# Second attention of a two-layer transformer kernel: moving the expert pieces behind the score rounds and spacing the two router calls

## The chip, the core and the metric

The kernel runs on one core of a Trainium2 chip. The core has a matrix engine (PE, with its weight loads shown apart as PEld), a vector engine (DVE), an activation engine (ACT), a general engine (POOL) and a queue engine that issues most transfers (SP). Each works through its own list of instructions in order, and waits on semaphores for the others. The metric is the device time of one execution in microseconds, the median of several runs; lower is better.

## The reference, cut to what matters

Two layers, each an attention with 16 heads of width 8 and then a mixture of 8 experts, of which each token takes 2. There are 64 batches of 128 tokens of width 128, all in float32. The change is in the second layer:

```python
x = x + _L0_xattn_ref(_layernorm(x), fside_BxSxS_0, ctx_1024, ctx_1024, ...)
x = x + _L0_ffn_ref(_layernorm(x), ...)
x = x + _L1_xattn_ref(_layernorm(x), ctx_1024, ctx_1024, ...)
x = x + _L1_ffn_ref(_layernorm(x), ...)
...
# _L1_xattn_ref, 120 keys a batch
scores = jnp.einsum('bhqd,bhkd->bhqk', Q, K) / jnp.sqrt(jnp.asarray(d, Q.dtype))
attn = jax.nn.softmax(scores, axis=-1)
out = jnp.einsum('bhqk,bhkd->bhqd', attn, V)
...
# _L1_ffn_ref
logits = xf @ Wg.T + bg
top_gates, top_idx = jax.lax.top_k(logits, K)
top_gates = jax.nn.softmax(top_gates, axis=-1)
h = jax.nn.gelu(jnp.einsum('nd,erd->enr', xf, W1), approximate=False)
eout = SCALING * jnp.einsum('enr,edr->ned', h, W2)
sel = jnp.take_along_axis(eout, top_idx[:, :, None], axis=1)
out = jnp.sum(top_gates[:, :, None] * sel, axis=1)
```

## The kernel before, in words

All 64 batches stay in on-chip memory as 16 groups of 4 (`xg`, `GB = 4`, `NG = 16`). The kernel runs through three stages: the first attention with the first router beside it, the first layer's experts as a stage of sorted tiles (`tile_stage`, L934), and the second attention (`attention(1, ...)`, called at L1278), beside which the second layer's router and experts run. The order of instructions on PE, DVE, ACT and POOL is the order in which the Python code writes them (`manual_schedule`).

**One iteration of the second attention** (the loop at L484; 69 iterations for 64 batches, since the stages of a batch are spread over iterations) does, for different batches at once:

- `values` and `out1` (L408, L424): softmax weights times values for batch `it-3`, 16 matmuls in L417; ACT copies the result (`ov`, L426).
- `rounds(0, 1)` (L384): for batch `it` the score matmuls whose row maxima are wanted (L344, 16 of them, banks that DVE reduces in L356), woven with those of batch `it-2` in transposed form (L372, 8 of them, banks that ACT turns into exponentials in L380). Four banks go to DVE and four to ACT.
- `prep` (L303): in turn over four iterations, keys (L188), values and the turned input (L199, L165), queries (L269) of the next group.
- `out3`, `out2`, `out4` (L446, L433, L453): transposes and the output projection; between them DVE computes `rs` and `o` (L437, L439).
- `shift` (L397): two transposes of the maxima (L401), which DVE adds into the queries (L404), so that the next iteration's L372 and L380 work on shifted scores.
- `out5`, `ahead`, `norm_of`, `fetch_for`: residual adds and statistics on DVE (L458, L116, L117), and on POOL the normalization of coming groups (L144 to L156) and the gathers of the first layer's expert results (`yb`, L1157, two indirect transfers an iteration), which are added to `x` (L1169).
- Then `aside.call` twice in a row (L545, L546).

**PSUM** is one pool of 8 banks (L225). A matmul that opens a bank waits until the bank's last reader is done; which bank it gets follows from the order in which the code takes and gives them up.

**The router** (`Router`, L559) is three generators that are driven by `call`; a counter `t` goes up by one at each call, and each generator says at which `t` it is due again. `front` (L596) runs per group: at `2 * (4 g + made_at)` statistics and normalization on POOL, at `2 * (4 g + at)` four transposes on PE and one ACT copy (`turned`, L162), and one call later the four logit matmuls (L615) that read that copy, with a DVE copy of the logits (L619). With `when = (8, 9)` (L1147) the turn and the logits stand back to back at the end of iteration `4 g + 9`. `back` (L625) then takes top-2 and gates in small DVE steps, one step a call (L712, L652 to L684, L1203 and L1204).

**The experts** (`experts`, L1209) are a generator with four pieces a group. A: the gates transposed (L1218), copied by ACT, and four matmuls of 512 columns (L1225), whose banks ACT passes through Gelu (L1228; ACT then has to load another table, and the exponentials' table again before the next L380). B: 16 small matmuls that spread the gates over four banks (L1235), by which DVE multiplies `h` (L1240, four times 512 columns). C twice: 8 matmuls back to width 128 (L1246) and a DVE add (L1251), the second time with the transfer out. `Aside1.call` (L1258) steps the router and, at every second call, the experts: one piece an iteration, as the last thing in it. What is left after the loop is done in `rest` (L1265).

Of the kernel before, what the change touches and what calls it, by code (L numbers as in the profile page):

```python
# [28 lines left out]
E = 8  # L29
# [15 lines left out]
def transformer_kernel(ctx, tc, a, out):  # L45
# [24 lines left out]
    def load_const(name, shape, src):  # L70
        t = const.tile(shape, F32, name=f"c_{name}", tag=f"c_{name}")
        nc.sync.dma_start(t, src)
        return t
# [94 lines left out]
    norms = [Norm(n) for n in range(4)]  # L168
# [48 lines left out]
    def attention(layer, w, norm, first, aside):  # L217
# [5 lines left out]
        with ExitStack() as es:  # L223
# [34 lines left out]
            def prep_x(g):  # L258
                xnT = work.tile([D, GB * S], F32, name="xnT", tag="xnT", bufs=1)
                norm.turned(normed.pop(g), mtile(), xnT)  # L260
                xnTs[g] = xnT
                q4s[g] = work.tile([128, GB, NS, S], F32, name="q4", tag="q4", bufs=3)
# [3 lines left out]
            def prep_q(g, v):  # L266
                if v == 0:
                    pqs[g] = mtile()
                    nc.tensor.matmul(pqs[g], lhsT=w["wq"], rhs=xnTs[g], start=True, stop=True)  # L269
                pq = pqs[g]  # L270
                for i in range(2):
                    s = 2 * v + i
                    nc.scalar.activation(  # L273
                        q4s[g][:, :, s, :], pq.rearrange("p (b q) -> p b q", b=GB),
                        AF.Identity, bias=w["bq"][:, s : s + 1], scale=hmask[:, s : s + 1],
                    )

            def prep_k(g):
                keys_of(w, src[g], g, n0, mtile())

            def prep_v(g):
                values_of(w, src[g], g, n0, mtile())
# [20 lines left out]
            def prep(it, half):  # L303

                g, j = it // GB + 1, it % GB
                if not first:
                    if g == 1:
                        if (j, half) == (2, 1):
                            prep_v(1)
                        elif (j, half) == (1, 0):  # L310
                            prep_k(1)
                    elif g < NG:
                        pieces = (
                            (), (lambda: prep_k(g),),
                            (lambda: prep_v(g), lambda: prep_x(g)),
                            (lambda: prep_q(g, 0), lambda: prep_q(g, 1)),
                        )[j]
                        if half < len(pieces):
                            pieces[half]()
                    return  # L320
                if (it, half) == (0, 1):
                    norm_of(1)
                    prep_x(1)
                if (j, half) == (3, 1):
                    if g + 1 < NG:
                        prep_x(g + 1)
                elif g >= NG:
                    return
                elif j == 0 and it or it == 1:
                    prep_q(g, half)  # L330
                elif (j, half) == (2, 0):
                    prep_k(g)
                elif (j, half) == (2, 1):
                    prep_v(g)
# [49 lines left out]
            def round_(ba, bc, rnd):  # L384


                one, two = ((0, 2), (1, 3)) if rnd % 2 == 0 else ((1, 3), (0, 2))
                left = [max_bank(ba, ra, rnd // 2) for ra in one] if ba is not None else []
                right = [score_bank(bc, ra, rnd // 2) for ra in two] if bc is not None else []
                banks = [x for pair in zip(left, right) for x in pair] if left and right else left + right  # L390
                for u in range(2):
                    for parts, _ in banks:
                        parts[u]()
                for _, after_ in banks:
                    after_()
# [65 lines left out]
            def norm_of(g):  # L461
                if g < NG:
                    normed[g] = norm.normed(g)

                    nc.gpsimd.tensor_tensor(
                        xg[g], xg[g], w["bo"].unsqueeze(1).to_broadcast([S, GB, D]), ALU.add
                    )
# [16 lines left out]
            for it in range(B + (4 if first else 5)):  # L484
                def on(back, *steps):
                    b = it - back
                    if 0 <= b < B:
                        for f in steps:
                            f(b)

                def rounds(*which):
                    ba = it if it < B else None
                    bc = it - 2 if 0 <= it - 2 < B else None
                    for r in which:
                        if ba is not None or bc is not None:
                            round_(ba, bc, r)

                if first and it % GB == 2:
                    norm_of(it // GB + 2)
                if 2 <= it <= B + 1:  # L500
                    ps_[it - 2] = work.tile([128, nc_, 4, 512], F32, name="p", tag="p")
                on(3, lambda b: values(b, 0), lambda b: values(b, 1), out1)
                if it % GB == 0 and 0 < it // GB + 1 < NG:
                    if it:
                        loads(it // GB + 1)
                if it % GB == 2 and it // GB + 1 < NG:
                    context(it // GB + 1)
                rounds(0, 1)
                if first:

                    on(3, out2)
                    prep(it, 0)
                    rounds(2, 3)
                    on(1, shift)
                    on(3, out3)
                    aside.call(it, mtile)
                    on(4, out4, out5)
                    aside.ahead(it)
                    prep(it, 1)
                    aside.call(it, mtile)  # L520
                    aside.end(it, work, mtile)
                else:
                    if it < GB - 1:
                        prep_batch(it + 1)
                    prep(it, 0)
                    on(4, out3)
                    on(3, out2)
                    on(5, out4)
                    prep(it, 1)
                    on(1, shift)  # L530
                    on(5, out5)
                    aside.ahead(it)
                    if it == GB - 1 or it > GB and it % GB == 1:
                        norm_of(it // GB + 1)
                    if it == 1:

                        nc.gpsimd.tensor_tensor(
                            xg[0], xg[0], w["bo"].unsqueeze(1).to_broadcast([S, GB, D]), ALU.add
                        )
                    if it == GB - 1:  # L540
                        prep_x(1)
                        prep_q(1, 0)
                        prep_q(1, 1)
                    aside.fetch_for(it)
                    aside.call(it, mtile)  # L545
                    aside.call(it, mtile)  # L546
                ps_.pop(it - 3, None)
                yield
# [10 lines left out]
    class Router:  # L559
# [15 lines left out]
        def call(self, probe, mtile):  # L575
            self.mtile, self.probe = mtile, probe
            self.t += 1
            for k, gen in enumerate(self.gens):
                if self.due[k] <= self.t:
                    self.due[k] = next(gen, 1 << 30)  # L580
# [529 lines left out]
    rp = ctx.enter_context(tc.tile_pool(name="route", bufs=1))  # L1110
# [9 lines left out]
    wr1 = load_const("wgT", [D, E], a["wgT"])  # L1120
# [14 lines left out]
    class Aside1:  # L1135


        def __init__(self, pool):
            self.pool, self.got, self.b, self.xn = pool, {}, 0, None
            self.xnTs, self.gates, self.ready = {}, [], []  # L1140
            for k in range(2):
                t = pool.tile([S, QM, 32], F32, name=f"gates_{k}", tag=f"gates_{k}")
                nc.gpsimd.memset(t, 0.0)  # L1143
                self.gates.append(t)
            parts = [(2 * k, 2 * k + 1) for k in range(GA // 2)] + [(g,) for g in range(GA, NG)]
            self.router = Router(
                rp, 1, norms[3], E, wr1, logits1, self.weigh, self.xnT_of, parts, (8, 9)  # L1147
            )
            self.work = self.experts()

# [105 lines left out]
                    yield  # L1256

        def call(self, it, mtile):  # L1258
            self.mtile = mtile
            self.router.call(None, mtile)  # L1260
            self.half = not getattr(self, "half", True)
            if self.half:
                next(self.work, None)

        def rest(self, mtile):  # L1265
            self.mtile = mtile
# [101 lines left out]
```

## Time and profile before

| what | value |
|---|---|
| median of 5 runs (lowest, highest) | 1624.65 us (1619.04, 1628.79) |
| profiled execution, its own time | 1631.8 us |
| its span, first to last instruction | 1630.0 us |
| mean granted clock of the matrix engine | 0.954 |
| second attention with its tail, about | from 1000 us to the end |
| stretch 1140 to 1580 us: PE, DVE, ACT, POOL busy | 406.20, 295.99, 250.89, 192.34 us |
| the same stretch: granted clock | 0.94 |

The profile is of one execution. Its views name an instruction by engine, line and operation, with its tiles written as "out <- in" and its shapes as partitions by elements. A list of waits puts idle time of an engine down to what ended it. A timeline gives start, length and, in brackets, the idle time ahead of an instruction and what released it. A table of windows gives the busy time of each engine in a stretch, then the clock that was granted to the matrix engine (PEclk, 1.00 is full speed). Matrix instructions are pipelined, and their ends are modelled.

### The profile page before, as it was taken

How to read it: one execution, taken by the hardware profiler on the slowest of the kernel's cores; microseconds unless marked ns; L12 is line 12 of the kernel's file. 1: busy time of each engine (PE TensorE's matmuls, PEld its weight loads, DVE VectorE, ACT ScalarE, POOL GpSimd, SP SyncE). 2: the span in 40 equal slices, each digit the busy share in tenths (PEclk: the TensorE clock that was granted, in tenths of full speed). 3: DMA queues.
4: the chain of work that ended last, by engine and by line, in shares of the span. 5: the costliest groups of instructions: out<-in, count | busy, mean ns of one | idle time of the engine just before them, and what ended most of it. 6: DMA issues, size and time to landing. Idle time of an engine off the chain costs nothing.

```text
span 1630.0 us, 44916 instructions
## 1 busy us (share of the span) xinstructions
PE 1474.4 (90%) x18156; PEld 1176.0 (72%) x18156; DVE 1059.9 (65%) x2923; ACT 838.7 (51%) x1722; POOL 641.5 (39%) x1211
## 2 busy tenths in 40 slices
PE   5999999999999998879999994788989899899997
PEld 3777777777776776868888883567767676677765
DVE  4778887878788875545544442467665666667854
ACT  3666665656565655423333332445555565556652
POOL 5124265555555545640000005575454555543200
PEclk9999999999999999999999995798998898999998
DMA  7411122222222221667766751110001111110000
GB/s 190 104 45 45 45 62 57 60 58 59 59 76 56 76 51 58 181 173 211 198 193 190 193 169 43 28 36 24 27 28 27 28 35 26 35 30 15 15 8 27
DMA packets 124130, 123.91 MB, mean 76 GB/s; under 512 B 47122, under 2 KB 106514, under 8 KB 122002
## 3 DMA queue, kind: packets, MB, share of 16 engines
q1 hardware_dynamic: 115730, 103.71, 23.8%
q0 software_dynamic: 8192, 17.32, 3.5%
q8 instruction: 144, 2.36, 0.6%
q14 instruction: 64, 0.52, 0.1%
HBM read 97.31 MB, written 23.67 MB: 74 GB/s over the span
## 4 chain that ended last, share of the span: by engine, by line
PE 76%; DVE 7%; ACT 5%; DMA 4%; issue 3%; POOL 2%; SPq 1%; another core or an unknown queue 1%; ACTq 0%; POOLq 0%; DVEq 0%
PE bank L372 15%; PE bank L417 12%; PE bank L344 12%; PE bank L997 9%; PE bank L1225 4%; PE bank L1246 4%; PE bank L1010 3%; DVE nm L356 3%; PE bank L401 2%; DMA q<-xs 2%; PE bank L433 2%; PE bank L269 2%; PE bank L615 2%; ACT p L380 2%; DMA vc<-xs 2%
## 5 line engine op out<-in xcount | busy, mean ns | idle before, releaser
L356 DVE TENSOR_REDUCE nm<-bank 128x2 f32<-128x496 f32 (+1 forms) x768 | 464.6, 663 | 244.4 <-PE bank L372 133.0
L372 PE MATMUL bank<-q,k 32*120 32x256 f32 (+1 forms) x3072 | 479.7, 417 | 13.0 <-ACT ov L426 4.8
L344 PE MATMUL bank<-k,q 32*128 32x248 f32 (+1 forms) x4096 | 463.6, 351 | 2.8 <-ACT q L298 1.1
L380 ACT ACTIVATE p<-bank 120x512 f32<-120x512 f32 (+1 forms) x768 | 402.9, 602 | 121.3 <-PE bank L372 78.0
L344 PEld LDWEIGHTS bank<-k,q 32*128 32x128 f32 x4096 | 361.9, 198 | 65.5 <-issue 28.2
L372 PEld LDWEIGHTS bank<-q,k 32*120 32x120 f32 (+1 forms) x3072 | 305.9, 186 | 41.5 <-DVE nm L356 15.4
L417 PE MATMUL bank<-p,v 128*32 128x128 f32 (+1 forms) x4096 | 199.5, 283 | 16.2 <-issue 13.1
L1002 DVE TENSOR_TENSOR p<-p,bank 128x256 f32<-128x256 f32 x213 | 88.1, 420 | 139.0 <-ACT p L1001 121.8
L426 ACT COPY ov<-bank 128x256 f32<-128x256 f32 x128 | 47.4, 371 | 236.9 <-PE bank L417 191.4
L417 PEld LDWEIGHTS bank<-p,v 128*32 128x32 f32 (+1 forms) x4096 | 122.8, 112 | 54.3 <-issue 33.8
L751 POOL DMA_INDIRECT xs<-xn,at x128 | 128.9, 1007 | 54.5 <-issue 30.6
L1157 POOL DMA_INDIRECT yb<-ys,back x128 | 123.7, 966 | 32.2 <-issue 28.0
L1001 ACT ACTIVATE p<-bank 128x256 f32<-128x256 f32 x213 | 80.7, 384 | 105.8 <-PE bank L997 103.0
L997 PE MATMUL bank<-q 128*128 128x256 f32 x516 | 120.8, 384 | 2.9 <-ACT e L675 1.8
L404 DVE SCALAR_TENSOR_TENSOR q<-bank,c_smask,q 128x256 f32<-128x256 f32 x256 | 111.1, 475 | 10.3 <-remote 4.2
L417 PE MATMUL bank<-p,vc 120*32 120x128 f32 x2048 | 114.3, 273 | 2.3 <-issue 2.1
L156 POOL TENSOR_SCALAR xn<-x,mv,rstd 128x128 f32<-128x128 f32 x256 | 111.2, 447 | 11.1 <-PE bank L165 5.2
L144 POOL TENSOR_SCALAR rstd<-mv 128x4 f32<-128x4 f32 (+1 forms) x33 | 6.5, 198 | 273.6 <-DVE mv L117 187.6
L997 PEld LDWEIGHTS bank<-q 128*128 128x128 f32 x516 | 95.8, 192 | 14.8 <-ACT e L675 2.1
L1143 POOL MEMSET gates<- 128x256 f32 x2 | 0.6, 311 | 250.2 <-DMA ys<-q 250.2
L273 ACT ACTIVATE q<-bank,c_a_bq,c_hmask 128x512 f32<-128x512 f32 x124 | 89.7, 781 | 13.3 <-PE bank L269 13.3
L997 PE MATMUL bank<-vc 128*128 128x256 f32 x336 | 78.8, 385 | 0.0
(201 smaller groups left out, 2284.9 us busy)
## 6 DMA issues: line engine op xcount, KB each, us to landing
q<-in_w SPq DMA_DIRECT2D x43, 576.0 KB
vc<-in_w SPq DMA_DIRECT2D x28, 576.0 KB
vc<-in_ctx_v SPq DMA_DIRECT2D x16, 960.0 KB
k<-in_ctx_k SPq DMA_DIRECT2D x32, 240.0 KB
q<-xs SPq DMA_DIRECT2D x43, 128.0 KB
ys<-q SPq DMA_DIRECT2D x43, 128.0 KB
x<-in_x SPq DMA_DIRECT2D x16, 256.0 KB
kvT<-in_fsideT SPq DMA_DIRECT2D x16, 256.0 KB
```

The source lines that it names most:

```text
L156: nc.gpsimd.tensor_scalar(xn[:, j, :D], xg[g][:, j, :], self.mv[:, b, 0:1], self.rstd[:, b : b + 1], ALU.add, ALU.mult,)
L273: nc.scalar.activation(q4s[g][:, :, s, :], pq.rearrange("p (b q) -> p b q", b=GB), AF.Identity, bias=w["bq"][:, s : s + 1], scale=hmask[:, ...
L344: nc.tensor.matmul(pa[:, u, :], lhsT=q4s[g][r, j, s, :], rhs=k2[g % 2][r, s // 2, j, :], start=True, stop=True,)
L356: nc.vector.tensor_reduce(nm[b % 2].rearrange("q i (a s) -> q a i s", s=16)[:, 2 * ra + v : 2 * ra + v + len(slots) // 2, :, 0], pa.rearra ...
L372: nc.tensor.matmul(pb[:n, v * 256 : (v + 1) * 256], lhsT=k2[g % 2][r, v, j, k0 : k0 + n], rhs=q4s[g][r, j, 2 * v : 2 * v + 2, :].rearrange ...
L380: nc.scalar.activation(ps_[b][:n, c, ra, :], pb[:n], AF.Exp, scale=SCALE)
L404: nc.vector.scalar_tensor_tensor(q, pm, smask[:, v : v + 1], q, ALU.mult, ALU.add)
L417: nc.tensor.matmul(pav[32 * ra : 32 * ra + 32, v * S : (v + 1) * S], lhsT=vs[g % 2][c][:, j, 4 * v + ra, i, :], rhs=p[:n, c, ra, (2 * v + ...
L751: s = nc.gpsimd.indirect_dma_start(xs, bass.IndirectOffsetOnAxis(at[:, j, k : k + 1], 0), xn, None)
L997: nc.tensor.matmul(ph[:, u, :], lhsT=w[:, c, u * 128 : (u + 1) * 128], rhs=xT, start=True, stop=True)
L1002: nc.vector.tensor_tensor(hT[:, c, :], sa, ph[:, 1, :], ALU.mult)
L1157: nc.gpsimd.indirect_dma_start(y[:, k, b % 2, :], None, ys, bass.IndirectOffsetOnAxis(back[:, b, k : k + 1], 0),)
```

## The change

The expert piece is taken out of `Aside1.call` into a method of its own, `piece`, which is called once an iteration directly after the rounds, before `prep`. One of the two router calls moves to the middle of the iteration, between `out4` and the second half of `prep`; the other stays at the end. The router's two due times move by half an iteration, `(8, 9)` to `(8.5, 9.5)`: the normalization and the turn stay at the end of iterations `4 g + 8` and `4 g + 9`, and the logits come in the middle of iteration `4 g + 10`. All else is as it was.

```diff
                 else:
+                    aside.piece(mtile)
                     if it < GB - 1:
                         prep_batch(it + 1)
                     prep(it, 0)
                     on(4, out3)
                     on(3, out2)
                     on(5, out4)
+                    aside.call(it, mtile)
                     prep(it, 1)
                     on(1, shift)
                     on(5, out5)
...
                     aside.fetch_for(it)
-                    aside.call(it, mtile)
                     aside.call(it, mtile)
...
             self.router = Router(
-                rp, 1, norms[3], E, wr1, logits1, self.weigh, self.xnT_of, parts, (8, 9)
+                rp, 1, norms[3], E, wr1, logits1, self.weigh, self.xnT_of, parts, (8.5, 9.5)
             )
...
         def call(self, it, mtile):
+            self.router.call(None, mtile)
+
+        def piece(self, mtile):
             self.mtile = mtile
-            self.router.call(None, mtile)
-            self.half = not getattr(self, "half", True)
-            if self.half:
-                next(self.work, None)
+            next(self.work, None)
```

In the built order of PE's instructions, an iteration that ended "... out4, shift, turn, logits, piece A" becomes "values, rounds, piece A, prep, out3, out2, out4, logits, turn, shift", one iteration later; B, C and C follow in the three iterations after it, each directly behind the rounds. The number of instructions of each engine is the same, POOL's order is the same, and SP's is too. On DVE the multiplications of B and the adds of C now stand between the four reductions (L356) and `rs`, `o` and the shift (L437, L439, L404); before, they stood at the iteration's end. On ACT the Gelu of A stands directly behind the four exponentials instead of at the iteration's end.

## The prediction

> **What bounds the kernel now.** I read the page first, then tables of windows cut at the iterations of the second attention, then timelines and waits of single engines there.
>
> ```profile
> PE 1474.4 (90%) x18156; PEld 1176.0 (72%) x18156; DVE 1059.9 (65%) x2923; ACT 838.7 (51%) x1722; POOL 641.5 (39%) x1211
> ...
> PEclk9999999999999999999999995798998898999998
> ...
> PE 76%; DVE 7%; ACT 5%; DMA 4%; issue 3%; POOL 2%; SPq 1%; another core or an unknown queue 1%; ACTq 0%; POOLq 0%; DVEq 0%
> ```
>
> PE is busy for 90% and carries 76% of the chain that ended last, so what the change is worth is read from PE: its idle time, and stretches at a lower clock. The clock row is full until slice 24 and dips in the last 16 of 40, nearly all of them the second attention, which is changed. I cut that part at the first L417 of each iteration. A group takes four iterations, those of pieces A, B, C, C. An undisturbed group late in the stage:
>
> ```profile
> 1510.80:1521.90 11.10, 10.18 (x111) 6.83 (x110) 7.54 (x30) 7.71 (x15) 6.56 (x15) 1.00 0.08 26
> 1521.90:1529.00 7.10, 7.07 (x136) 6.11 (x135) 4.58 (x12) 4.96 (x9) 1.11 (x1) 1.00 0.00 0
> 1529.00:1536.90 7.90, 7.90 (x109) 6.56 (x109) 7.39 (x20) 5.01 (x10) 0.00 (x0) 1.00 0.02 4
> 1536.90:1542.90 6.00, 6.00 (x105) 5.45 (x104) 5.28 (x17) 3.08 (x7) 0.00 (x0) 1.00 0.00 0
> ```
>
> Columns: stretch, length, then PE, PEld, DVE, ACT, POOL busy, granted clock, transfers. The group takes 32.1 us, PE is busy for 31.15 of it, and the clock is full. DVE's 24.79 is not far behind. Four iterations out of two groups in the middle of the stage:
>
> ```profile
> 1413.30:1420.70 7.40, 7.28 (x136) 6.09 (x137) 4.50 (x11) 4.96 (x9) 6.37 (x7) 1.00 0.24 62
> 1420.70:1433.70 13.00, 11.16 (x110) 8.51 (x112) 8.28 (x23) 5.03 (x10) 5.32 (x7) 0.74 0.10 26
> ...
> 1439.80:1453.40 13.60, 11.79 (x111) 7.54 (x110) 7.76 (x30) 7.91 (x15) 8.69 (x16) 0.87 0.07 21
> 1453.40:1462.60 9.20, 8.44 (x136) 6.99 (x136) 4.07 (x10) 5.05 (x9) 7.65 (x9) 1.00 0.26 70
> ```
>
> The same instructions take 13.00 instead of 7.90 and 13.60 instead of 11.10. These two groups (1402.2 to 1477.6) take 75.4 us against 2 x 32.1 = 64.2: some 11 us in 75 are lost, to waits and to a clock of 0.74 and 0.87. So the stage has three payers: PE's work, PE's waits, and the clock. The iteration with A shows the waits that the change aims at:
>
> ```profile
> 1444.91 0.60 PE L165 MATMUL bank<-ident,xn 128*128 128x128 f32 x4
> 1446.43 1.06 PE L615 MATMUL bank<-c_wgT,xnT 128*128 128x8 f32 x8 [0.92 <-ACT xnT L166]
> 1448.38 0.45 PE L1218 MATMUL bank<-ident,gates 128*128 128x128 f32 x1 [0.89 <-DVE lg L619]
> 1448.62 4.87 PE L1225 MATMUL bank<-xnT,c_lw1T 128*128 128x512 f32 x8
> ```
>
> The turn's copy on ACT holds the logits up for 0.92 us, and the bank of the gates' transpose waits 0.89 us for DVE. Then L1225 takes 4.87 us; in groups at full clock it takes 3.60.
>
> **What goes.** (1) The logits come half an iteration after the turn: values, rounds, piece A and `out3` to `out4` of the next iteration lie between, over 8 us, against ACT's copy of 0.6 us. PE's waits from 1140 to 1580 us:
>
> ```profile
> PE bank L615 <- ACT xnT L166: 12.0, 13, 1.2
> ...
> PE bank L1218 <- DVE lg L619: 4.4, 5, 0.9
> ```
>
> 12.0 us of the first kind go; the same list from 1060 to 1140 has 1.3 us more, in two waits. The last group's, 1.23 us in the tail, stays, since there turn and logits still follow each other. (2) The gates' transpose no longer follows the logits: 4.4 us. (3) If those waits are what lowers the clock in A, that goes too: 100 matmuls of L1225 are busy for 53.6 us in that stretch, 12.5 pieces at 3.60 would be 45.0, so at most 8.6 and at least 0; I take 6, since the slow pieces are those with both waits. Sum: 12.0 + 1.3 + 4.4 + 6 = 24 us.
>
> The Trainium skill, "TensorE: Matmul & The Clock Gate", Part 1, says that the clock halves after a whole idle window of about 3.4 us. Two waits of 0.9 us with matmuls between are not such a window, and by that rule item 3 would be 0 and the sum 18. The rows show 4.87 us behind exactly such a pair of waits and 3.60 behind a single one, so I keep 6.
>
> **What comes.** (4) B's 16 matmuls open four banks at once, and directly behind the rounds these are the rounds' first banks: two that DVE reduces and two that ACT reads in L380 (the order of allocation in the built program gives this). ACT has just done A's Gelu and must reload its table ahead of L380:
>
> ```profile
> 1524.24 1.28 ACT L380 ACT_TABLE_LOAD   x1 [0.75 <-PE bank L344]
> 1525.54 2.06 ACT L380 ACTIVATE p<-bank 120x512 f32<-120x512 f32 x4
> ```
>
> This load waits for the first finished bank, so it is not hidden early. The rounds start at 1522.9 here and end 2.3 us later on PE; the second exponential is done at 1525.54 + 2.06 / 2 = 1526.57, 3.65 us after that start. Today PE has keys, values and transposes to do meanwhile. With B next in line it stands 3.65 - 2.3 = 1.3 us, and everything behind B on PE with it. The load is not new: it stands in the iteration behind A today too, but no matmul needs those banks so early. Bounds: 0 where a halved clock makes PE late itself, 1.9 if a third exponential had to end. 13 pieces B in the loop: 17 us.
>
> (5) B's products are now ahead of the shift on DVE:
>
> ```profile
> 1527.86 0.88 DVE L404 SCALAR_TENSOR_TENSOR q<-bank,c_smask,q 128x256 f32<-128x256 f32 x2 [0.24 <-PE bank L401]
> ...
> 1529.69 2.47 DVE L1240 TENSOR_TENSOR h<-h,bank 128x512 f32<-128x512 f32 x4
> 1532.08 2.35 DVE L356 TENSOR_REDUCE nm<-bank 128x4 f32<-128x480 f32 x4
> ```
>
> From B's last matmul DVE needs 2.47 + 0.25 (L437) + 0.29 (L439) + 0.87 (L404) = 3.9 us to finish the shifted queries, which the next rounds need. PE fills this with the queries' projection 1.1, the output steps and the shift 0.9 and the values 1.1, together 3.1. It stands 0.8 us: 13 x 0.8 = 10 us. (6) The adds of C (0.40 each) wait for C's 1.95 us of matmuls and stand ahead of `rs`, `o` and the shift; PE's own steps behind C nearly cover that, and I charge 0.2 x 26 = 5. Router steps that now stand ahead of the shift (L666 to L669, 0.64 us, and two of 0.2) cost up to 0.6 in each of nine chains: 5. Sum: 17 + 10 + 5 + 5 = 37.
>
> (7) Given back: today L1240 runs at 1529.69, ahead of the next reductions at 1532.08, and in that iteration, the one of 7.90, the rounds end 3.35 us after their start instead of 2.3, since DVE frees their banks late. That 1.0 us goes: 13 us.
>
> Net: -24 + 37 - 13 = 0 us. Own time 1631.8 + 0. That execution lay 7.15 us over the median, so on the median's scale I put 1624.65 + 0, and 1626 as a round number.
>
> (8) **The unknown.** POOL's gathers come in a row, and PE does badly beside them:
>
> ```profile
> 1421.07 0.94 POOL L1157 DMA_INDIRECT yb<-ys,back  x1 [0.30 <-issue]
> 1422.32 0.95 POOL L1157 DMA_INDIRECT yb<-ys,back  x1 [0.30 <-issue]
> ```
>
> Four run from 1418.56 to 1423.27. In that time PE's L417, issued behind B from 1420.66, stops three times (0.32, 0.44 and 1.02 us, released by nothing that the profile shows), the products of B wait 2.27 us, and then the clock halves. Without gathers, at 1528.97, the same L417 runs in 1.08 us. The Trainium skill, "SBUF — State Buffer", SBUF: two separate sides, says that PE never waits on another user of the memory; by that rule the stop would belong to B itself and move with it, and nothing would be added or taken for (8). Before the experts begin there is no B, yet at 1093.54 to 1098.24 four gathers cost a shift 2.54 us of waiting, so I tie it to the gathers. They are released by statistics at the end of the iteration ahead of A now, that is C's second after the change, some 2 us later in that iteration; the row of four should then meet values, rounds and B. What it costs there no row shows: today two groups pay 11 us, less 3.5 for items 1 to 3, so 7.5, in some 4.5 such pairs: 34 us; I take the same. Bounds: half to two thirds of it hidden under A's long matmuls, with items 5 and 6 at half (10), is -27 to -32; another 3.4 us at half clock in each of 13 groups, 1.7 x 13, is +22, and +25 with the third exponential in a few.
>
> **The rivals.** *Even* (forecast, 36%): -10 to +10, about 1626. *Slower* (31%): the gathers hit rounds and B while PE already stands for the table load and the shift; PE's idle time in that iteration grows from 2.1 us past some 3, and the clock halves in each group. It decides where C's second iteration ends its statistics so late that the row of four begins with the values. Price 1.7 x 13 = +22: 1648. For it: the 0.74 at 1420.7. Against: at 1453.4 a row of four left the clock at 1.00. *Faster* (33%): the gathers fall on A and `out4`, whose consumers have slack, and half of the 34 us goes, with 10 of items 5 and 6: -27, 1599. For it: A has the most cover of all pieces. That the change is not carried out is excluded: the built order shows the pieces and calls in their new places in all groups.
>
> **Chances and range.** Within 0.5% (about 8 us, what a measurement here can tell from no change): 0.30. Faster: 0.33. Slower: 0.37, the rival and the upper edge of the forecast. The range 1590 to 1651 takes in both bounds of (8).
>
> **What would show it.** Right: no wait of L615 on L166 in the loop; a wait of L1235 on L380's exponentials of about 1.3 us, 13 times; L372 waiting for L404 about 0.8 us behind B; L1225 at 3.60 throughout. Wrong: L1235 without a wait; iterations with B under 8 us; a clock below 0.94 or above 0.98 in the stage.

## The result, and the profile after

The changed kernel takes **1630.64 us** (median of 42 runs, 1626.72 to 1635.89) where the kernel before takes 1626.51 (79 runs, 1615.79 to 1635.23): a ratio of **1.0028, 95% interval 1.0018 to 1.0038**. A second comparison gave 1.0020 (1.0001 to 1.0039). The forecast of 1626 within 0.5% held. The profiled execution took 1630.17, its span is 1628.4 (before 1631.8 and 1630.0).

The page, the lines that answer to those of before:

```profile
PE 1486.1 (91%) x18156; PEld 1187.8 (73%) x18156; DVE 1060.6 (65%) x2923; ACT 837.8 (51%) x1722; POOL 643.5 (40%) x1211
...
PEclk9999999999999999999999995799999988889999
...
PE 74%; DVE 10%; DMA 5%; issue 4%; ACT 3%; POOL 2%; SPq 1%; another core or an unknown queue 0%; POOLq 0%; ACTq 0%; DVEq 0%
```

The clock row moved a little, and it is coarse: a slice lasts 41 us, and a 9 stands for 90% or more. Over 1140 to 1580 us the granted clock is 0.92, where it was 0.94. In each of the first nine groups it is halved once, for 6.8 us (10.2 us in one), the first time at 1154 us. So something still happens once a group. Line numbers of the changed kernel are 3 higher from L559 on (logits L618, gates' transpose L1221, A L1228, B L1238 and L1243, C L1249, gathers L1160). In the table of windows, iterations A and B of a group in the middle, then B of a late group without gathers:

```profile
1438.90:1449.00 10.10, 9.97 (x118) 7.39 (x116) 6.35 (x22) 7.37 (x17) 7.24 (x12) 1.00 0.17 43
1449.00:1463.70 14.70, 13.36 (x126) 9.64 (x127) 7.45 (x19) 5.65 (x10) 7.88 (x9) 0.69 0.13 35
...
1523.50:1531.20 7.70, 7.35 (x126) 5.75 (x129) 5.88 (x14) 4.89 (x9) 0.00 (x0) 1.00 0.01 2
```

A's iteration is 10 us long, at full clock, here and in all groups of the loop, where it was 13.6 and 11.1 before. B's iteration is 14.7, at a clock of 0.69, where it could be 7.7. In the first nine groups it takes 13.0 to 14.6 us, and eight of the nine groups take 37.5 to 38.1 us, as most do before. PE's waits from 1140 to 1580 us:

```profile
PE bank L372 <- issue: 5.3, 13, 0.9
PE bank L1249 <- DVE nm L356: 4.6, 7, 0.8
PE bank L1238 <- DVE nm L356: 4.1, 4, 1.7
PE bank L344 <- issue: 2.0, 7, 0.4
PE bank L372 <- DVE q L404: 1.8, 1, 1.8
PE bank L1238 <- ACT p L380: 0.9, 3, 0.3
PE bank L1238 <- issue: 0.8, 3, 0.3
```

The two waits that the change aims at are gone from the loop. At the top now stands "issue": matmuls of the rounds that nothing in the profile holds up. Such waits are not new. In the kernel before, the same list has them at the values and at B, that is, on other work:

```profile
PE bank L417 <- issue: 7.8, 10, 1.1
...
PE bank L1235 <- issue: 2.3, 6, 0.5
```

Together they were 10.1 us and are 8.1 now, so the waits alone do not tell the cost. POOL's timeline in front of and beside that B:

```profile
1449.86 0.96 POOL L1160 DMA_INDIRECT yb<-ys,back  x1
1451.14 0.94 POOL L1160 DMA_INDIRECT yb<-ys,back  x1 [0.31 <-issue]
1452.39 0.95 POOL L1160 DMA_INDIRECT yb<-ys,back  x1 [0.30 <-issue]
1453.64 0.94 POOL L1160 DMA_INDIRECT yb<-ys,back  x1 [0.30 <-issue]
```

The row of four lies beside the rounds of B's iteration, which take 6.8 us here instead of 2.3; towards their end, at 1454.5, the clock halves. POOL runs these gathers in one go because they stand in its list behind the normalization of the next group, which waits up to 14.1 us for statistics of DVE (L117; up to 15.0 before).

### The profile page after: what moved, and what is told of

Read it like the earlier page. It is cut to its first block, busy times and chain, and to the rows that moved or that the text cites. A ratio compares the mean times of both kernels' runs of the same rounds, so it can differ in the third digit from the quotient of the medians.

```text
span 1628.4 us, 44848 instructions
## 1 busy us (share of the span) xinstructions
PE 1486.1 (91%) x18156; PEld 1187.8 (73%) x18156; DVE 1060.6 (65%) x2923; ACT 837.8 (51%) x1722; POOL 643.5 (40%) x1211
## 4 chain that ended last, share of the span: by engine, by line
PE 74%; DVE 10%; DMA 5%; issue 4%; ACT 3%; POOL 2%; SPq 1%; another core or an unknown queue 0%; POOLq 0%; ACTq 0%; DVEq 0%
PE bank L372 14%; PE bank L344 11%; PE bank L417 11%; PE bank L1000 9%; PE bank L1249 4%; DVE nm L356 4%; PE bank L1228 3%; PE bank L1013 3%; DMA q<-xs 2%; PE bank L269 2%; PE bank L1238 2%; PE bank L433 2%; PE bank L401 2%; PE bank L187 2%; PE bank L618 2%
## 5 line engine op out<-in xcount | busy, mean ns | idle before, releaser
L356 DVE TENSOR_REDUCE nm<-bank 128x2 f32<-128x496 f32 (+1 forms) x768 | 463.1, 662 | 184.1 <-PE bank L372 113.6
L344 PEld LDWEIGHTS bank<-k,q 32*128 32x128 f32 x4096 | 356.9, 190 | 80.3 <-issue 39.7
L372 PEld LDWEIGHTS bank<-q,k 32*120 32x120 f32 (+1 forms) x3072 | 300.6, 182 | 46.6 <-DVE nm L356 15.7
L417 PE MATMUL bank<-p,v 128*32 128x128 f32 (+1 forms) x4096 | 191.2, 280 | 10.1 <-issue 5.9
L426 ACT COPY ov<-bank 128x256 f32<-128x256 f32 x128 | 47.8, 373 | 205.9 <-PE bank L417 155.6
L1160 POOL DMA_INDIRECT yb<-ys,back x128 | 124.0, 969 | 32.2 <-issue 25.8
L404 DVE SCALAR_TENSOR_TENSOR q<-bank,c_smask,q 128x256 f32<-128x256 f32 x256 | 111.2, 476 | 12.1 <-PE bank L401 9.0
```

What stands on the lines that cost most here:

```text
L344: nc.tensor.matmul(pa[:, u, :], lhsT=q4s[g][r, j, s, :], rhs=k2[g % 2][r, s // 2, j, :], start=True, stop=True,)
L356: nc.vector.tensor_reduce(nm[b % 2].rearrange("q i (a s) -> q a i s", s=16)[:, 2 * ra + v : 2 * ra + v + len(slots) // 2, :, 0], pa.rearra ...
L372: nc.tensor.matmul(pb[:n, v * 256 : (v + 1) * 256], lhsT=k2[g % 2][r, v, j, k0 : k0 + n], rhs=q4s[g][r, j, 2 * v : 2 * v + 2, :].rearrange ...
L404: nc.vector.scalar_tensor_tensor(q, pm, smask[:, v : v + 1], q, ALU.mult, ALU.add)
L417: nc.tensor.matmul(pav[32 * ra : 32 * ra + 32, v * S : (v + 1) * S], lhsT=vs[g % 2][c][:, j, 4 * v + ra, i, :], rhs=p[:n, c, ra, (2 * v + ...
L1160: nc.gpsimd.indirect_dma_start(y[:, k, b % 2, :], None, ys, bass.IndirectOffsetOnAxis(back[:, b, k : k + 1], 0),)
```

## The experiments

Theory G: the gathers (L1160) disturb PE, the change moves them from values and shift onto rounds and B, and the half clock that follows there eats what A gained. Rival T: the place of the piece itself (table load, banks, DVE's order) costs the time. The comparisons fell on several chips, on which the kernel before takes 1542 to 1627 us; each ratio below is to the kernel before on the same chip.

**The parts alone.** `calls_only` takes the piece back to the iteration's end; `piece_only` takes the calls back.

```diff
 # calls_only
-                    aside.piece(mtile)
...
                     aside.call(it, mtile)
+                    aside.piece(mtile)
 # piece_only
-                    aside.call(it, mtile)
...
                     aside.call(it, mtile)
+                    aside.call(it, mtile)
...
-                ..., parts, (8.5, 9.5)
+                ..., parts, (8, 9)
```

> The two router calls are apart, with (8.5, 9.5), and the pieces stay at the end of an iteration. Theory G (POOL's gathers, four in a row, meet the rounds and piece B in the changed kernel and halve the clock there): the logits' and gates' waits go, the gathers stay where they are, so the gain of 18 to 24 us shows: 1603 to 1610. Theory T (the pieces' place costs through the table load and banks) says the same here. Rival W (the waits in A only covered other waits, such as DVE behind piece A): 1620 or more. If B in this kernel takes 13 us too, the calls alone move the gathers.

> The piece stands behind the rounds, both router calls are at the end, with (8, 9). Theory G: the logits' wait stays (12 us), the gathers still meet rounds and B, so this is the changed kernel plus about 12: 1640 to 1646. Theory T the same. If the place of the calls, and not that of the pieces, moves the gathers onto the rounds: B's iteration takes about 8 us here and the time lies below 1620.

Both ran on the chip with 1542.26 us. `calls_only`: 1535.46, ratio 0.9954 (0.9938 to 0.9971). `piece_only`: 1560.43, 1.0121 (1.0105 to 1.0137). The first gains less than expected, since A at the end of the iteration now waits for gates that the same call has only just made:

```profile
PE bank L1221 <- DVE gates L1207: 11.7, 4, 2.9
```

That is 2.9 us in every second group (A's iteration 12.7 or 14.4 instead of 9.0). The time of `piece_only` came out near what was expected: L618 waits for the turn's copy again (0.92 each), and the rounds wait up to 1.30 us for ACT's `ov` (L426), eight times, which was not foreseen. The surprise lies elsewhere: on this chip B's iteration takes 7.7 to 7.8 us in both kernels, and neither has an "issue" wait, though the gathers run as ever, in rows of up to four. So these runs say nothing on G yet.

**Without gathers.** The same bytes come on SP's queue, as consecutive rows (not those of the tokens):

```diff
-                    nc.gpsimd.indirect_dma_start(
-                        y[:, k, b % 2, :], None, ys,
-                        bass.IndirectOffsetOnAxis(back[:, b, k : k + 1], 0),
-                    )
+                    nc.sync.dma_start(
+                        y[:, k, b % 2, :], ys[(2 * b + k) * S : (2 * b + k + 1) * S]
+                    )
```

> The changed kernel with the indirect gathers of the first layer's expert rows replaced by plain transfers of consecutive rows on SP's queue, so the rows added to x are not those of the tokens. Theory G: B's iteration falls from 13 to 14.6 us to about 7.7, the clock between 1140 and 1580 us goes from 0.92 to 1.00, a group takes 31.4: about 11 x 6.2 = 68 us less, 1560 to 1570. Theory T (table load, banks, and DVE's order ahead of the shift cost the time, whatever POOL does): B's iteration stays over 11 us and the time over 1600.

> The kernel before with the same plain transfers in place of the gathers (the rows added to x are not those of the tokens). Theory G: a group falls from 37.5 to about 32.1, so 11 x 5.4 = 59 us less, and some 10 more from the early rows: 1560 to 1575, so that with the gathers gone the change is worth -15 to 0. Theory T: the kernel before loses nothing to gathers and stays over 1610; and the changed kernel is the slower one by 17 us or more when both are without them.

On the chip with 1542: 1515.96 (0.9832, 0.9819 to 0.9845) and 1529.04 (0.9912, 0.9899 to 0.9925). The changed kernel is then the faster by 13 us. Rival T, by which B's iteration would stay over 11 us, is out: it takes 7.67 us, though B stands behind the rounds. But the expected 60 us were not to be had here, where gathers do less harm. Hence the same two kernels on chips where they do:

> The changed kernel with plain transfers of consecutive rows in place of the gathers (the rows added to x are not those of the tokens), once more. If the kernel before takes 1627 here and PE stalls beside gathers: theory G says that with the gathers gone B's iteration is 7.7 us in every group and a group takes 32, so 5.5 x 10 = 55 us less than the changed kernel, 1575, ratio 0.968. Rival D (PE is disturbed by any transfer into on-chip memory, or by the place itself): B's iteration stays over 10 us, ratio above 0.985. If the kernel before takes 1542 here: a repetition, ratio 0.983.

> The kernel before with plain transfers in place of the gathers (the rows added to x are not those of the tokens), beside the runs in which the changed kernel with the same edit had a ratio of 0.953. Theory: without gathers the change is worth what the runs at 1542 showed, 13 us, so 0.961, about 1562 where the kernel before takes 1627; and the gathers cost the kernel before some 65 us and the changed one some 80 us. Rival (the change gains nothing by itself, whatever the gathers do): 0.953, as the changed kernel. Second rival (the gathers cost both kernels the same): 0.950, since before and after are 0.3% apart with them.

The changed kernel without gathers: **1544.99, ratio 0.9528** (0.9479 to 0.9577; kernel before 1624.53). The kernel before without them: **1556.82, 0.9646** (0.9633 to 0.9659; before 1613.37 on yet another chip). The gain is larger than G expected for the changed kernel; 20 us of it come from iterations 1 to 14, which G's sum left out. The change alone is worth 0.9528 / 0.9646 = 0.988 across these two chips, and 1515.96 / 1529.04 = 0.991 on the one with 1542. The changed kernel's windows, A and B of one group, in the form used above:

```profile
1328.70:1338.60 9.90, 9.90 (x121) 7.40 (x124) 5.37 (x16) 7.27 (x16) 7.25 (x12) 1.00 0.09 24
1338.60:1346.20 7.60, 7.25 (x122) 5.67 (x121) 6.17 (x16) 4.79 (x8) 0.00 (x0) 1.00 0.19 52
```

B's iteration has 7.6 us at full clock, in all groups alike, with the transfers right beside it (0.19). No "issue" wait is left. In the kernel before without gathers, A still shows its two waits and the half clock behind them (L1217 and L1224 are its gates' transpose and A):

```profile
1249.35 1.06 PE L615 MATMUL bank<-c_wgT,xnT 128*128 128x8 f32 x8 [0.92 <-ACT xnT L166]
1251.29 0.30 PE L1217 MATMUL bank<-ident,gates 128*128 128x128 f32 x1 [0.89 <-DVE lg L619]
1251.43 5.30 PE L1224 MATMUL bank<-xnT,c_lw1T 128*128 128x512 f32 x8
```

**Both kernels once more**, on a chip where the kernel before takes 1627.26:

> The changed kernel as it is, beside the runs in which the kernel before took 1542 us instead of 1627 and PE did not stall beside the gathers. Theory G2 (the rounds' and B's stalls beside the gathers are a matter of the run's surroundings, and the change moves them from one place to another): where PE is not disturbed, B's iteration takes 7.7 us as without gathers, and the time is that of the kernel with plain transfers, 1516 to 1522, a ratio of 0.983 to 0.987. Rival: B's iteration takes 13 us here too, because this kernel's place for the gathers is the bad one: 1570 to 1580, ratio 1.02.

> The kernel before once more, for its trace: by G2, A's iterations of 11.1 and 13.6 us stay, the others are those of the kernel with plain transfers (7.1, 8.0 to 8.4, 6.0), and no matmul waits 'for issue' beside the gathers. By the rival the iterations of 9.2 and 13.0 that the first profile shows are there again.

1629.91 and 1627.8. The rival of this expectation was right in that B's iteration takes 12.3 to 14.6 us in the changed kernel here; theory G2 holds only in that the chip matters. Cutting the stage at the iterations gives the account (spans in the profiles of `before`, `after`, `before_plain_b` and `after_plain_b`; the kernels without gathers have the same middle row within 0.1 us on two chips each):

| PE's iterations | before | after | before without gathers | after without |
|---|---|---|---|---|
| 1 to 14 (no experts) | 113.0 | 106.5 | 89.5 | 86.2 |
| 15 to 61 | 429.4 | 430.9 | 393.9 | 378.4 |
| 62 to the end | 63.7 | 68.0 | 61.2 | 68.4 |

In the middle row the gathers cost 429.4 - 393.9 = 35.5 us before and 430.9 - 378.4 = 52.5 after. The 28 us between the two runs of the kernel before without gathers (1529 and 1557) lie ahead of the second attention, which starts at 983 us on the one chip and at 1016 on the other.

**The gathers moved.** In `after_paced` a small POOL copy of the iteration's `rs` holds each pair back, so that four never run in a row. In `after_on_a` the gathers are to run beside A, released by the gates' copy.

```diff
 # after_paced, in fetch, ahead of each pair
+                if probe is not None:
+                    nc.gpsimd.tensor_copy(spacer, probe)
 # after_on_a, in experts, piece A
                 nc.scalar.copy(gT, pt)
+                self.fetch(3, gT[0:1, 0:1])
```

> The changed kernel with each pair of gathers held back by a small POOL copy of the iteration's rs, so that two run in each iteration behind the rounds and four never run in a row. By G2 nothing moves where PE is not disturbed: within 0.3% of the changed kernel of the same call. By the rival (the row of four is what costs) B's iteration falls to 7.7 us and the time by 50 us or more against the changed kernel.

> The changed kernel with the eight gathers of a group moved: six are released by the copy of the gates in piece A, and so run beside A's long matmuls and what follows them, two by rs of C's second iteration. This is the case that the prediction called faster: gathers on A are hidden. By it A's iteration stays at 10 us, B's falls to 8 to 9, a group takes 32 to 33, 45 us less than the changed kernel where that takes 1630: 1585, ratio 0.975. Rival (gathers halve the clock wherever they run): A's iteration grows to 14 or more, no gain.

`after_paced`: 1618.25, 0.9948 (0.9916 to 0.9980), far from the 50 us: with rows of two B's iteration still takes 9.3 to 12.0. `after_on_a`: 1631.14, 1.0044 (1.0020 to 1.0068). It did not test what it should: the gathers stand behind the normalization in POOL's list. In the group looked at they started at 1411.81, 2.3 us after the gates' copy was done, and six in a row ran on into the rounds of B's iteration (11.8 to 16.9 us).

**Another order.** Calls apart, the piece at the end but ahead of the second call (the call of `piece` behind the rounds goes), first alone and then with pairs held back:

```diff
                     aside.fetch_for(it)
+                    aside.piece(mtile)
                     aside.call(it, mtile)
```

> The calls apart as in the change, the piece at the end of the iteration, but ahead of the second call. With the calls alone, A's gates come 2.9 us too late in every second group, and a half clock follows (iterations of 12.7 and 14.4 instead of 9.0); here A finds its gates made one iteration earlier. Theory: all groups take 31.0 us, so about 4.5 us less in each of five or six: 1535 - 25 = 1510. Rival (DVE is behind by then and another wait takes the place): 1525 or more.

> The kernel with the calls apart and the piece at the end ahead of the second call (ratio 0.985), with each pair of gathers held back by a small POOL copy of the iteration's rs. In the changed kernel this pacing gave 0.7%. Theory G: the same here, 0.975 to 0.980. Rival: pairs meet the rounds of every iteration instead of four meeting one, and it gives nothing: 0.985 or more.

`piece_ahead_of_call`: **1605.59, 0.9846** (0.9818 to 0.9874). A's gates are always there, A's iteration is 9.9 us in every group; the gathers still meet B's rounds (10.6 to 12.6). `best_paced`: **1577.21, 0.9718** (0.9655 to 0.9781), faster than both kernels. A and B of one of its groups:

```profile
1368.30:1378.20 9.90, 9.90 (x120) 7.30 (x120) 6.02 (x18) 6.91 (x13) 8.81 (x15) 1.00 0.23 66
1378.20:1385.70 7.50, 7.27 (x122) 5.75 (x121) 4.54 (x13) 5.83 (x11) 2.49 (x4) 1.00 0.08 20
```

The gathers are all there, and the clock is full; the two iterations with C behind them take 8.1 and 7.6 us, at full clock too. Of waits that nothing in the profile explains, 3.3 us are left from 1060 to 1540 us, nearly all at the values. Pairs alone did not do this in `after_paced`. As I read the timelines, what differs is where `rs` falls. With the piece at the end, `rs` comes early, and the pairs run beside the output steps, the piece and the values. With the piece behind the rounds, `rs` comes late, and they run into the next rounds. Counted in the traces over seven groups (iterations 19 to 46; the 56 gathers take 54 to 55 us in each kernel; the rounds count from their first matmul to the end of their last):

| kernel | gather time beside rounds | longest row | the seven groups |
|---|---|---|---|
| before | 18.4 | 4 | 263.4 |
| after | 27.4 | 4 | 263.2 |
| `after_paced` | 31.2 | 2 | 256.1 |
| `piece_ahead_of_call` | 24.4 | 4 | 254.8 |
| `best_paced` | 6.8 | 2 | 229.5 |
| after without gathers | 0 | 0 | 225.2 |
| `calls_only` (chip with 1542) | 19.0 | 4 | 229.8 |

A disturbed round is longer, so part of the second column follows from the fourth; the step from 31.2 to 6.8 does not. Two reservations stand against the overlap as the measure of the harm. In the kernel before, a pair of gathers lies beside 2.1 us of the rounds in every second group, and these rounds last 2.32 us, as without gathers:

```profile
1414.48 1.10 POOL L1157 DMA_INDIRECT yb<-ys,back  x1 [0.17 <-issue]
1415.88 0.95 POOL L1157 DMA_INDIRECT yb<-ys,back  x1 [0.30 <-issue]
```

The row of four that follows there (1418.56 to 1423.27) meets B and the values, and the values take 4.7 us instead of 1.08. And the last line: on that chip 19.0 us of overlap left no wait without a releaser and a B's iteration of 7.8 us in every group. So that the gathers cost the time is shown, by the kernels without them; that it is the overlap with the rounds is argued.

## Why the prediction was right, point by point

The time was right, and by luck: errors as large as 17 us cancel. Without gathers each term can be set beside the traces: two groups of each kernel, iterations 27 to 34 before and 28 to 35 after, each kind of PE work counted from the end of the work ahead of it to its own end. The forecast's sums are divided by 13 groups, (1) without its 1.3 us ahead of 1140 us. Matmuls overlap, and where one kind ends and the next begins is good to about 0.1 us; the sum is not touched by that.

| step | forecast, us a group | measured |
|---|---|---|
| (1) logits' wait | -0.92 | -1.18 |
| (2) gates' wait | -0.34 | -0.31 |
| (3) A at half clock | -0.46 | -0.85 |
| (4) B waits for the exponentials' banks | +1.31 | +1.36 |
| (5), (7) rounds behind B: late shift, banks given back | +0.77 - 1.00 | -0.54 |
| (6) C's adds, router steps | +0.77 | +0.78 |
| seams: keys, values, output steps, shift | 0 | -0.79 |
| sum | +0.13 | -1.53 |

- **(1) and (2)** held; the waits are gone from the loop. **(3)** held for A, which takes 3.60 throughout the loop, and was set too low: without gathers the slow A follows the pair of waits in four of five groups (in both runs of that kernel), as the rows of before suggested, and never the first wait alone. In the fifth the same two waits leave A at 3.60. 0.92 and 0.89 us of waiting with matmuls between are no whole idle window of 3.4 us, so the rule of the Trainium skill ("TensorE: Matmul & The Clock Gate", Part 1) would have left A at full clock; the measurement differs, and it decides.
- **(4)** was right in cause and size, and the sign that I named for it was wrong. ACT's table load stands exactly where the prediction put it, in the changed kernel without gathers:

```profile
1309.25 1.28 ACT L380 ACT_TABLE_LOAD   x1 [0.75 <-PE bank L372]
1310.54 2.06 ACT L380 ACTIVATE p<-bank 120x512 f32<-120x512 f32 x4
```

  And B in PE's timeline of the same kernel (B is L1237 there):

```profile
1309.98 0.90 PE L1237 MATMUL bank<-gT,c_select 32*128 32x128 f32 x4
1311.19 1.64 PE L1237 MATMUL bank<-gT,c_select 32*128 32x128 f32 x28 [0.31 <-ACT p L380]
```

  Only 0.31 us shows as a wait of PE, twelve times in the loop. The rest is in the stretch: B's 16 matmuls (32 in the profile) last from 1309.98 to 1312.83, 2.85 us, and 1.3 in the kernel before. That the table load makes this stretch is read from the two timelines; no run takes the load away.
- **(5)** likewise: the rounds behind B last 3.1 us instead of 2.3, the 0.8 that was charged, of which 0.2 at most is listed as a wait for L404. **(7)** gave back 1.3 instead of 1.0: before, those rounds last 3.4 and 3.8 us without gathers.
- **(6)** met its size (0.78 for 0.77), in part by another wait: C's second iteration waits 0.76 us for DVE's reductions (L356) in every second group.
- **The seams**, small steps on which no wait had been charged, were not in the sum at all, and they are the largest miss outside (8). The output steps give 0.45 of it, the keys and the values' projection 0.2 each. As I read it, they stood a little for ACT and DVE right behind the rounds, and with the piece ahead of them their operands are there; no run takes that apart.
- **(8)**, "I take the same", is the step that failed. "34 us today" was right (35.5). After the change it is 52.5: +17, inside the bound of +22, by the mechanism of the *slower* rival, down to the place: the row of four begins with the values of B's iteration, and the clock halves there in each disturbed group. That rival's price was near (22 for 17) and its base was not: it added 22 to a net of 0, and the net of the rest is -15.5 in the loop. The step said that the gathers would cost the same at their new place without a row that showed it.
- **The tail** was left out of the sum. It costs 4.3 us with gathers and 7.2 without: the second-last rounds wait 1.78 us for the shift (step (5) once in full), and the last turn waits for POOL's normalization, whose statistics now stand behind C's adds and router steps on DVE (read from DVE's list, not tested):

```profile
1563.25 1.24 PE L372 MATMUL bank<-q,k 32*120 32x256 f32 x8 [1.78 <-DVE q L404]
...
1590.38 1.78 PE L165 MATMUL bank<-ident,xn 128*128 128x128 f32 x4 [3.14 <-POOL xn L156]
```

In sum, for the profiled pair: iterations 1 to 14 -6.5 (not taken apart here); the loop -15.5 + 17.0 = +1.5; the tail +4.3; together -0.7, beside -1.6 between the spans. By the medians the changed kernel is 4.1 us slower, so this account of a single pair is good to some 6 us.

- **The signs.** Of those named for being right two came (no wait of the logits in the loop, A at 3.60) and two did not (B's wait of 1.3 us, and 0.8 us for L404). Of those named for being wrong two came: a clock of 0.92 in the stage, which the half clock behind the gathers makes, and iterations with B under 8 us. The latter was a poor sign, since an undisturbed B's iteration takes 7.67 us with the cost of (4) in it.
- **The rule on the memory's sides** (the Trainium skill, "SBUF — State Buffer", SBUF: two separate sides) was weighed against (8). The same bytes, brought into the same buffers by SP's queue, leave no "issue" wait and a clock of 1.00 in the loop. For these transfers the runs agree with that rule. What disturbs PE is the gathers, and whether they do it in the memory is open. The consequence that I drew from the rule and then set aside, that the stop would belong to B, is refuted: B without gathers has none.

**Open:** by what way a gather on POOL holds PE up, and why on one chip it does not. No run here separates the work of POOL from the scattered reads or from the queue that carries them. Everything on the chip with 1542 us was measured at one time, so a trait of that chip and a passing state of it are not told apart. The changed kernel itself was not run there.

## What to carry to other kernels

Cut a moved step's account at the iterations and look at every engine that free-runs beside it: POOL's list had not changed by one instruction, and still its burst fell on other work, since the wait that released it ended at another point. A small copy that ties background transfers to a chosen point of each iteration took the ratio from 0.985 to 0.972 with the piece at the iteration's end, and from 1.002 to 0.995 with the piece behind the rounds; so the point matters as much as the copy. And when a forecast holds, take the terms apart all the same: here -6.5, -15.5, +17.0 and +4.3 made it.

## What the runs showed of the hardware

- Beside rows of four indirect gathers of 128 rows on POOL (0.95 us each), PE's rounds last 4.6 to 6.8 us instead of 2.3 in the changed kernel. Only 0.2 to 1.2 us of that is listed as waits, without a releaser, and a half clock of 6.8 us follows in eight of nine groups. Plain transfers of the same bytes do nothing of the kind, and a pair of gathers left rounds beside it at 2.32 us in the kernel before.
- The chips, or their states at the time, differ in it: on one, 19.0 us of the same gathers lay beside rounds, and B's iteration took 7.8 us in every group.
- The clock halved behind two waits of 0.92 and 0.89 us that lay within 2 us of each other (A 5.1 to 5.3 us instead of 3.60) in four of five groups of the kernel before without gathers, and never behind the first alone. A single wait of 2.9 to 3.0 us ahead of A was followed by a half clock in three of five groups of `calls_only`.
- A table load on ACT took 1.28 us each time. The one ahead of the exponentials began only when their first bank was finished, though ACT had been idle for 0.75 us (kernels without gathers).
